# A graph attention layer and a multi-head attention layer on one core: layer 0's transformation from seven products of quarters, on normalized aggregates, with statistics on ScalarE and GpSimd

## The chip, the cores and the metric

The kernel runs on one core of a Trainium2 chip. The metric is the device time of one execution in microseconds (us). Before the change it is 2976.44 us, the median of 3 runs (2975.86 to 2976.45). The hardware profiler took one more execution, and all durations of rows in this text come from that one. The engines are TensorE (PE; its weight loads are PEld), VectorE (DVE), ScalarE (ACT), GpSimd (POOL) and SyncE (SP), which issues most DMAs.

## What is computed

`x` has 64 groups of 256 tokens with 512 features; `adj` is one 256 x 256 mask for all groups. Two layers follow each other, each on a normalized input and added to `x`:

```python
h = jnp.maximum(_layernorm(x, axis=-1), 0.0)
x = x + _L0_gnn_ref(h, adj, L0_gnn_W, L0_gnn_a_src, L0_gnn_a_dst)
h = jnp.maximum(_layernorm(x, axis=-1), 0.0)
x = x + _L1_gnn_ref(h, adj, L1_gnn_Wq, ..., L1_gnn_bo)
```

Layer 0 is a graph attention: `Wh = h W`, logits `leaky(Wh a_src + Wh a_dst)` between all pairs of tokens of a group, masked, softmax over the neighbours, times `Wh`. Layer 1 is multi-head attention with 8 heads of 64: projections with bias, scores scaled by 1/8, the same mask, softmax, values, output projection with bias. All is float32.

## The kernel before, in words

**Groups and stages.** The kernel works on one group (two token tiles of 128 tokens, `NT` = 2) at a time in each stage, and on several groups at once in different stages. Stages are Python generators; each `yield` ends a step. A hand-written list, `period` (L766) with `second` (L762), says in which order the steps of the stages are issued; it is run once per group `i`, and beside each stage stands how many groups ahead of `i` (or behind it) the step works. Every engine executes its instructions in the order in which they were issued, so this list is the order of the work on PE, VectorE, ScalarE, GpSimd and on SP's queue. Waits between engines follow from the data. The first period (`first`, L787), the steps ahead of it (L772 to L786) and `last` (L769) are written out too. The tiles of PSUM are eight banks, used in turn (`bank`, L139).

**Layer 0.** `normalize0` (two groups ahead, four steps): ScalarE sums x and the squares (L414, L420), VectorE scales the sums and adds epsilon (L417, L104), GpSimd raises to the power -0.5 (L106), VectorE forms the shift (L427), ScalarE normalizes and applies ReLU (L429); then VectorE multiplies with the two folded vectors `wa` and sums (L436), which gives the two terms of the logits. `weights0` (two steps): PE transposes one term over all rows (`pe`, L450), ScalarE takes two exponentials for the two branches of the leaky ReLU (L457, L458); then VectorE takes their maximum (L462), and GpSimd multiplies by the mask (`em`, L464) and adds the two halves (`esum`, L466). `aggregate0` (four steps): PE multiplies h by the weights (`pu`, L479) into the transposed aggregate, ScalarE copies it to `uT` (L486); in a third step PE sums `esum` over partitions (`ps`, L492), in a fourth VectorE takes the reciprocal `rs` (L496, L497). `transform0` (one group ahead, called W in the list, four steps, two per token tile): PE multiplies `uT` by the whole w (`po`, L508: per token tile four matmuls of 512 columns, each in two passes, so 8 rows), VectorE scales by `rs` and adds to x (L525).

**Layer 1.** `normalize1` (N1, three steps): VectorE's statistics (L99, L100, L104), GpSimd's power (L106), VectorE's shift (L540), ScalarE's normalization into `xn` (L545). `transpose1` (X1): PE transposes (`pt`, L561), ScalarE applies ReLU (L562), and GpSimd forms four sums of quarters, `hs` (`combine`, L165 to L168). `project_qk` (K), `project_v` (V) and `output` (O) each take seven products of quarters of the two operands in place of eight (`products`, L171). One product of K is 8 matmuls of 128 columns with two passes each; one of V or O is two matmuls of 256 columns with two passes each, hence 4 rows. VectorE adds each product to its destinations (`add_up`, L189; for O L727 straight to x, in pieces of 1024, 768, 256, 512, 512, 256 and 256 elements per partition). `attention` (A for group i, A_OLD for the one behind) has eight steps: scores of two head pairs (`psc`, L627) with ScalarE's exponential (L635); mask of one pair (VectorE: two multiplications L640 and a sum `sm` L642); mask of the other; values (`pav`, L652) with ScalarE's copy; the same four for the other two head pairs. The last of them also lets GpSimd add the bias to x (L671), sums over partitions (`psm`, L679), takes the reciprocal (`rc`, L687) and issues eight small DMAs on SP that spread it over partitions. `scale` multiplies by it on VectorE (L704) and forms the sums of quarters `as` on GpSimd.

**The order around the change**, `second` from L762:

```python
        second = [
            K, O, A_OLD, A, E0, W, W, N1, V, E0, W, W, N1, V, V, N1, A, V, A,
            U0, V, V, U0, V, X1, X1, X1, U0, U0, A, A, (scale, -1),
        ]
```

E0 is `weights0`, U0 is `aggregate0`, both two groups ahead; `aside` puts steps of one-time checks (`constants`, among them the Gram products L333) between the others during the start.

Of the kernel before, what the change touches and what calls it, by code (L numbers as in the profile page):

```python
# [28 lines left out]
def kernel(  # L29
# [72 lines left out]
    def inverse_std(var, nm, small, scale=1.0):  # L102
        ve = small.tile([P, NT], F32, tag="ve", name=f"ve{nm}")
        nc.vector.tensor_scalar(ve, var, scale, EPS, op0=ALU.mult, op1=ALU.add)  # L104
        rstd = small.tile([P, NT], F32, tag="rstd", name=f"rstd{nm}")
        nc.gpsimd.tensor_tensor(rstd, ve, minus_half, op=ALU.pow)  # L106
        return rstd
# [24 lines left out]
    def bounded():  # L132
# [6 lines left out]
        def bank(shape, name):  # L139
            return ps_mm.tile(shape, F32, tag="mm", name=name)  # L140
# [90 lines left out]
        w_sb = weights.tile([P, DC, D], F32, tag="w_sb", name="w_sb")  # L231
        nc.sync.dma_start(w_sb, w.rearrange("(c p) e -> p c e", p=P))
# [4 lines left out]
        nc.gpsimd.dma_start(adj_sb, adj.rearrange("(c p) m -> p c m", p=P))  # L237
        load_group(1)
# [13 lines left out]
        def node_weights():  # L252
            wa_c = weights.tile([P, 2, DC], F32, tag="wa_c", name="wa_c")
            for c in range(DC):
                for j in range(2):
                    junk = work.tile([P, D], F32, tag="junk", name=f"junk_a_{j}_{c}")
                    nc.vector.scalar_tensor_tensor(
                        junk, w_sb[:, c, :], 1.0, a_rows[j], op0=ALU.mult, op1=ALU.mult,
# [143 lines left out]

        nodes, edges, sums0, lefts, norms, qkv, vs, outs = {}, {}, {}, {}, {}, {}, {}, {}

        def normalize0(g):
# [5 lines left out]
            nmean = small.tile([P, NT], F32, tag="nmean", name=f"nmean_{g}")  # L411
            ssq = small.tile([P, NT], F32, tag="ssq", name=f"ssq_{g}")
            for t in range(NT):
                nc.scalar.activation(  # L414
                    h[:, t, :], xt[:, t, :], AF.Copy, accum_out=nmean[:, t : t + 1]
                )
            nc.vector.tensor_scalar_mul(nmean, nmean, -1.0 / D)  # L417
            yield
            for t in range(NT):
                nc.scalar.activation(  # L420
                    h[:, t, :], xt[:, t, :], AF.Square, bias=nmean[:, t : t + 1],
                    accum_out=ssq[:, t : t + 1],
                )
            rstd = inverse_std(ssq, f"0_{g}", small, 1.0 / D)
            yield
            nmr = small.tile([P, NT], F32, tag="nmr", name=f"nmr_{g}")
            nc.vector.tensor_mul(nmr, nmean, rstd)  # L427
# [13 lines left out]
            nc.vector.tensor_scalar_mul(edl, ed, NEG_SLOPE)  # L441
# [3 lines left out]
        def weights0(g):  # L445
# [21 lines left out]
            edges[g] = em, esum  # L467
            yield

        def aggregate0(g):  # L470

            h = nodes.pop(g)[0]
            em, esum = edges.pop(g)
            uT = big.tile([P, DC, TOK], F32, tag="uT", name=f"uT_{g}")
            for dp in range(0, DC, 2):
# [10 lines left out]
                nc.scalar.copy(uT[:, dp : dp + 2, :], pu)  # L486
                yield

            rs = small.tile([P, NT], F32, tag="rs", name=f"rs_{g}")
            ps = bank([P, NT], f"ps_{g}")  # L490
            for t in range(NT):
                nc.tensor.matmul(  # L492
                    ps[:, t : t + 1], esum[:, t * P : (t + 1) * P], ones[:, 0:1], start=True, stop=True
                )
            yield
            nc.vector.tensor_scalar_max(rs, ps, 1e-38)  # L496
            nc.vector.reciprocal(rs, rs)  # L497


            sums0[g] = uT, rs  # L500
            yield

        def spread(ps, shape):
            return ps[:, 0:HD].unsqueeze(1).to_broadcast(shape)

        def project_half(dst, left, w_t, t, n):
            for c in (2 * n, 2 * n + 1):
                nc.tensor.matmul(  # L508
                    dst, left(c, t), w_t[:, c, :], start=(c == 0), stop=(c == DC - 1)
                )  # L510

        def transform0(g):

            xt = xts[g]
            uT, rs = sums0.pop(g)

            def left(c, t):
                return uT[:, c, t * P : (t + 1) * P]

            for t in range(NT):  # L520
                po = bank([P, D], f"po0_{g}_{t}")
                project_half(po, left, w_sb, t, 0)
                yield
                project_half(po, left, w_sb, t, 1)
                nc.vector.scalar_tensor_tensor(  # L525
                    xt[:, t, :], po, rs[:, t : t + 1], xt[:, t, :], op0=ALU.mult, op1=ALU.add
                )
                yield

        def normalize1(g):  # L530
            xt = xts[g]
            mv = small.tile([P, NT, 2], F32, tag="mv", name=f"mv1_{g}")
            for t in range(NT):
                token_stats(mv[:, t, :], xt[:, t, :], f"1_{g}_{t}", small)
                if t == 0:
                    yield
            rstd = inverse_std(mv[:, :, 1], f"1_{g}", small)
            yield
            nmr = small.tile([P, NT], F32, tag="nmr1", name=f"nmr1_{g}")
            nc.vector.scalar_tensor_tensor(  # L540
                nmr, mv[:, :, 0], -1.0, rstd, op0=ALU.mult, op1=ALU.mult
            )
            norms[g] = big.tile([P, NT, D], F32, tag="xn", name=f"xn_{g}")
            for t in range(NT):
                nc.scalar.activation(  # L545
                    norms[g][:, t, :], xt[:, t, :], AF.Identity,
                    bias=nmr[:, t : t + 1], scale=rstd[:, t : t + 1],
                )
            yield
# [17 lines left out]
        def project_qk(g):  # L567
# [6 lines left out]
            s2 = work.tile([P, 4, P], F32, tag="s2", name=f"s2_{g}")  # L574

# [3 lines left out]
            def read(n, ps):  # L579
# [6 lines left out]
                elif n == 4:  # L586
# [5 lines left out]
                    ps = p5  # L592
# [119 lines left out]
        def output(g):  # L712
            xt = xts.pop(g)
            a, s = outs.pop(g)
            quarters = xt.rearrange("p t (j d) -> p (t j) d", j=2)
# [296 lines left out]
```

## Time and profile before

| What | Value |
|---|---|
| median of the runs | 2976.44 us |
| the profiled execution | 2976.81 us |
| its span, first to last instruction | 2975.0 us |
| granted clock of TensorE, mean | 0.997 of full speed |
| VectorE busy | 2162.9 us (73%) |
| ScalarE busy | 1108.7 us (37%) |
| GpSimd busy | 907.0 us (30%) |
| transform of layer 0 on PE (L508) | 460.5 us, 1024 rows |
| VectorE's masks (L640) | 459.0 us, 512 rows, mean 937 ns |
| VectorE's shift of layer 0 (L427) | 72.2 us, 64 rows, mean 1129 ns |

The page gives for each engine the busy time, and for groups of instructions the source line, the operation, the tiles written and read, the count, and the mean duration of one. A timeline gives start, duration, engine, line and tiles of each instruction or of several alike in a row, and in brackets the idle time of the engine just before, with what ended it. A row of a matmul [...]overlaps the next row; so the time that a piece of PE work takes is read from start to start. A float32 matmul shows as two rows of MATMUL.

### The profile page before, as it was taken

Reading aid. Unit: us, or ns where it says so; the run is one execution under the profiler, and the core shown is the slowest. Engines: PE = TensorE matmul, PEld = TensorE weight load, DVE = VectorE, ACT = ScalarE, POOL = GpSimd, SP = SyncE. Lnnn points to the kernel's source line nnn. Section 1 sums busy time; section 2 is a strip of 40 time slices with the busy share of each in tenths; the row PEclk is TensorE's granted clock in tenths of the full one; section 3 lists DMA queues with packets and bytes.
Section 4 is the critical chain, followed back from the end, with each engine's and each line's share of the span. In section 5 each row is a group of like instructions: output and inputs, shape, how many; then the busy total and the mean of one; then the engine's idle time right before and its main releaser. Section 6 shows DMA issues by size and latency. Waiting matters only on the chain.

```text
span 2975.0 us, 48278 instructions
## 1 busy us (share of the span) xinstructions
PE 2930.9 (99%) x18942; PEld 2334.5 (78%) x18942; DVE 2162.9 (73%) x3858; ACT 1108.7 (37%) x2523; POOL 907.0 (30%) x920
## 2 busy tenths in 40 slices
PE   7999999999999999999999999999999999999997
PEld 5778778778788787787787787887877877878875
DVE  5777777777777777777777777777777777777766
ACT  4433434334343333334343333433333343433321
POOL 2223323223233233233232232332332332322322
PEclk9999999999999999999999999999999999999999
DMA  3121221221212212212212212122122122122122
GB/s 128 22 43 23 42 41 25 43 35 31 43 31 34 44 29 36 43 22 44 38 28 43 35 31 43 31 35 43 29 36 43 22 43 36 29 43 33 25 29 37
DMA packets 82714, 111.21 MB, mean 37 GB/s; under 512 B 11826, under 2 KB 48690, under 8 KB 82482
## 3 DMA queue, kind: packets, MB, share of 16 engines
q1 hardware_dynamic: 81682, 105.95, 22.3%
q8 instruction: 152, 2.49, 0.3%
q0 software_dynamic: 800, 2.11, 0.2%
q14 instruction: 80, 0.66, 0.1%
HBM read 40.90 MB, written 33.55 MB: 25 GB/s over the span
## 4 chain that ended last, share of the span: by engine, by line
PE 97%; DVE 2%; DMA 1%; POOL 0%; SPq 0%; issue 0%; ACT 0%; DVEq 0%; POOLq 0%
PE pqk L216 27%; PE po L508 15%; PE po L207 13%; PE pv L207 13%; PE psc L627 8%; PE pav L652 8%; PE pu L479 7%; PE psm L679 2%; PE pt L561 2%; PE pe L450 1%; PE ps L492 1%; DVE ex L640 0%; PE pgram L333 0%; DMA a_row<-in_L_gnn_a_dst_dram 0%; SPq L692 0%
## 5 line engine op out<-in xcount | busy, mean ns | idle before, releaser
L640 DVE TENSOR_TENSOR ex<-ex,maskT 128x512 f32<-128x512 f32 x512 | 459.0, 937 | 86.7 <-ACT ex L635 86.7
L508 PE MATMUL po<-w_sb,uT 128*128 128x512 f32 x1024 | 460.5, 592 | 0.0
L464 POOL TENSOR_TENSOR em<-e,maskT 128x512 f32<-128x512 f32 x64 | 81.0, 1265 | 1045.7 <-DVE e L462 1040.1
L525 DVE SCALAR_TENSOR_TENSOR x<-po,rs,x 128x512 f32<-128x512 f32 x128 | 96.1, 751 | 369.8 <-PE po L508 369.8
L508 PEld LDWEIGHTS po<-w_sb,uT 128*128 128x128 f32 x1024 | 189.6, 190 | 187.7 <-issue 184.1
L635 ACT ACTIVATE ex<-psc 128x512 f32<-128x512 f32 x512 | 264.4, 603 | 125.4 <-PE psc L627 125.4
L727 DVE TENSOR_TENSOR x<-po,x 128x256 f32<-128x256 f32 (+3 forms) x448 | 305.8, 683 | 6.7 <-PE po L207 6.5
L216 PEld LDWEIGHTS pqk<-hs,wq_sb 128*128 128x128 f32 x2048 | 268.3, 192 | 13.6 <-POOL hs L166 0.8
L216 PE MATMUL pqk<-hs,wq_sb 128*128 128x128 f32 x2048 | 270.0, 275 | 0.7 <-POOL hs L166 0.7
L216 PE MATMUL pqk<-hs,wk_sb 128*128 128x128 f32 x2048 | 270.5, 275 | 0.0
L207 PE MATMUL po<-wo_sb,as 128*128 128x256 f32 x1024 | 265.2, 382 | 4.4 <-POOL as L166 4.4
L660 ACT COPY aT<-pav 128x512 f32<-128x512 f32 x128 | 75.1, 587 | 514.6 <-PE pav L652 486.8
L207 PE MATMUL pv<-wv_sb,hs 128*128 128x256 f32 x1024 | 262.7, 379 | 0.0
L652 PE MATMUL pav<-ex,v 128*64 128x256 f32 x2048 | 251.6, 386 | 6.8 <-DVE ex L640 3.7
L627 PE MATMUL psc<-qk 64*128 64x256 f32 x2048 | 255.7, 389 | 0.0
L216 PEld LDWEIGHTS pqk<-hs,wk_sb 128*128 128x128 f32 x2048 | 249.3, 192 | 0.0
L479 PE MATMUL pu<-em,h 128*128 128x256 f32 x1024 | 243.2, 381 | 3.5 <-POOL em L464 3.5
L545 ACT ACTIVATE xn<-x,nmr,rstd 128x512 f32<-128x512 f32 x128 | 97.2, 806 | 389.7 <-DVE nmr L540 389.7
L627 PEld LDWEIGHTS psc<-qk 64*128 64x128 f32 x2048 | 187.3, 186 | 67.7 <-ACT aT L660 25.9
L207 PEld LDWEIGHTS pv<-wv_sb,hs 128*128 128x128 f32 x1024 | 194.9, 190 | 53.5 <-issue 29.9
L106 POOL TENSOR_TENSOR rstd<-ve,minus_half 128x2 f32<-128x2 f32 x128 | 90.4, 706 | 460.0 <-DVE ve L104 459.9
L165 POOL TENSOR_TENSOR hs<-hT 128x256 f32<-128x256 f32 x64 | 78.7, 1229 | 479.5 <-ACT hT L562 479.5
(166 smaller groups left out, 5252.3 us busy)
## 6 DMA issues: line engine op xcount, KB each, us to landing
x<-in_x_dram SPq DMA_DIRECT2D x64, 512.0 KB, 5.4
rb<-rc SPq DMA_DIRECT2D x512, 64.0 KB, 4.7
out_dram<-x SPq DMA_DIRECT2D x128, 256.0 KB, 2.0
w_sb<-in_L_gnn_W_dram SPq DMA_DIRECT2D x1, 1024.0 KB, 8.2
wq_sb<-in_L_gnn_Wq_dram SPq DMA_DIRECT2D x4, 256.0 KB, 13.4
wk_sb<-in_L_gnn_Wk_dram SPq DMA_DIRECT2D x4, 256.0 KB, 9.9
wo_sb<-in_L_gnn_Wo_dram SPq DMA_DIRECT2D x4, 256.0 KB, 6.6
wv_sb<-in_L_gnn_Wv_dram SPq DMA_DIRECT2D x4, 256.0 KB, 6.6
```

The lines of the kernel that those rows point to most:

```text
L106: nc.gpsimd.tensor_tensor(rstd, ve, minus_half, op=ALU.pow)
L207: nc.tensor.matmul(dst[:, 0:HD], left[:, c, :], wt[:, slot, c, :], start=c == 0, stop=c == 1)
L216: nc.tensor.matmul(dst[:, at : at + P], wt[:, slot, c, e * P : (e + 1) * P], left[:, c, :], start=c == 0, stop=c == 1,)
L479: nc.tensor.matmul(pu[:, d, :], h[:, m, (dp + d) * P : (dp + d + 1) * P], em[:, m, :], start=(m == 0), stop=(m == NC - 1),)
L508: nc.tensor.matmul(dst, left(c, t), w_t[:, c, :], start=(c == 0), stop=(c == DC - 1))
L525: nc.vector.scalar_tensor_tensor(xt[:, t, :], po, rs[:, t : t + 1], xt[:, t, :], op0=ALU.mult, op1=ALU.add)
L545: nc.scalar.activation(norms[g][:, t, :], xt[:, t, :], AF.Identity, bias=nmr[:, t : t + 1], scale=rstd[:, t : t + 1],)
L627: nc.tensor.matmul(psc[r][:, m, :], qk[rows, 2 + e % 2, m * P : (m + 1) * P], qk[rows, e % 2, :], start=True, stop=True,)
L635: nc.scalar.activation(ex[:, r, :, :], psc[r], AF.Exp, scale=SCALE)
L640: nc.vector.tensor_mul(ex[:, r, :, :], ex[:, r, :, :], maskT)
L652: nc.tensor.matmul(pav[r * DH : (r + 1) * DH, i, :], v[j][:, m, at : at + DH], pair[i][:, r, m, :], start=(m == 0), stop=(m == NC - 1),)
L727: nc.vector.tensor_add(dst, spread(ps, [P, dst.shape[1], HD]), dst)
```

## The change

- **Transformation from seven products.** `w_sb` is held as quarters (`load_quarters`) with their sums (`combine_w(w_sb)`), `aggregate0` ends with GpSimd's four sums of quarters of `uT` (`us`), and `transform0` runs `products` with `product_rows`, as O does; it has seven steps. `add_to_rows` is O's addition, now shared. The whole w, for the folded vectors, goes to two tiles that later hold `hT` and `xn`; w is thus loaded twice.
- **Normalized aggregates.** The row sum (`ps`) and its reciprocal `rs` are a third step of `weights0`; a fourth step transposes `rs` over all rows (`prs`) and ScalarE copies that to `rb0`. VectorE multiplies `pu` by `rb0` where ScalarE copied before.
- **Statistics.** A class `Stats` sums x (scaled by -1/D) and squares on ScalarE, and takes epsilon, power and shift on GpSimd. Both layers use it. `edl` goes to GpSimd.
- **Order.** W has seven steps, E0 four; masks 2 and 3 of the group behind (A_OLD) go from the start of the period to between the products K; the addition of K's product 4 waits until that of product 5 (`held`).

The core of the diff:

```diff
-        w_sb = weights.tile([P, DC, D], F32, tag="w_sb", name="w_sb")
-        nc.sync.dma_start(w_sb, w.rearrange("(c p) e -> p c e", p=P))
+        w_c = [big.tile([P, 2, D], F32, tag=tag, name=f"w_{tag}") for tag in ("hT", "xn")]
+        for i in range(2):
+            nc.sync.dma_start(w_c[i], w[i * HD : (i + 1) * HD, :].rearrange("(c p) e -> p c e", p=P))
...
+        w_sb = load_quarters(w, "w_sb")
         load_group(1)
...
+        class Stats:
...
+            def mean(self, t):
+                nc.scalar.activation(
+                    self.junk[:, t, :], self.xt[:, t, :], AF.Copy, scale=-1.0 / D,
+                    accum_out=self.nmean[:, t : t + 1],
+                )
+            def squares(self, t):
+                nc.scalar.activation(
+                    self.junk[:, t, :], self.xt[:, t, :], AF.Square, bias=self.nmean[:, t : t + 1],
+                    accum_out=self.ssq[:, t : t + 1],
+                )
+            def close(self):
...
+                nc.gpsimd.tensor_scalar(ve, self.ssq, 1.0 / D, EPS, op0=ALU.mult, op1=ALU.add)
+                nc.gpsimd.tensor_tensor(rstd, ve, minus_half, op=ALU.pow)
+                nc.gpsimd.tensor_tensor(nmr, self.nmean, rstd, op=ALU.mult)
+                return nmr, rstd
...
             nc.gpsimd.tensor_tensor(esum, em[:, 0, :], em[:, 1, :], op=ALU.add)
-            edges[g] = em, esum
+            yield
+            ps = bank([P, NT], f"ps_{g}")
+            for t in range(NT):
+                nc.tensor.matmul(
+                    ps[:, t : t + 1], esum[:, t * P : (t + 1) * P], ones[:, 0:1], start=True, stop=True
+                )
+            rs = small.tile([P, NT], F32, tag="rs", name=f"rs_{g}")
+            nc.vector.tensor_scalar_max(rs, ps, 1e-38)
+            nc.vector.reciprocal(rs, rs)
+            yield
+            pr = bank([P, N], f"prs_{g}")
+            for t in range(NT):
+                nc.tensor.transpose(
+                    pr[:, t * P : (t + 1) * P], rs[:, t : t + 1].to_broadcast([P, P]), ident
+                )
+            rb0 = work.tile([P, N], F32, tag="rb0", name=f"rb0_{g}")
+            nc.scalar.copy(rb0, pr)
+            edges[g] = em, rb0
             yield
...
-                nc.scalar.copy(uT[:, dp : dp + 2, :], pu)
+                nc.vector.tensor_mul(
+                    uT[:, dp : dp + 2, :], pu, rb0.unsqueeze(1).to_broadcast([P, 2, N])
+                )
...
+            sums0[g] = a, combine(a, ("us", str(g)))
+            yield
...
         def transform0(g):
+            a, s = sums0.pop(g)
+            yield from products(
+                a, s, f"po0_{g}", partial(product_rows, w_sb), partial(add_to_rows, xts[g])
+            )
...
         def normalize1(g):
+            stats = Stats(xt, xn, f"1_{g}")
+            stats.mean(1)
+            stats.squares(1)
+            yield
+            stats.mean(0)
+            stats.squares(0)
+            nmr, rstd = stats.close()
+            yield
...
         second = [
-            K, O, A_OLD, A, E0, W, W, N1, V, E0, W, W, N1, V, V, N1, A, V, A,
-            U0, V, V, U0, V, X1, X1, X1, U0, U0, A, A, (scale, -1),
+            N0, A_OLD, A, E0, W, W, W, V, E0, A, W, W, V, E0, W, N1, W, E0, N1, V, V, A, U0, N1,
+            V, V, U0, V, X1, X1, X1, A, A, (scale, -1),
         ]
         period = [
-            (load, 3), A_OLD, K, A_OLD, O, K, N0, O, K, N0, O, K, N0, O, K, O, N0, K, O,
+            (load, 3), K, O, K, N0, O, (aggregate0, 1), K, N0, O, K, A_OLD, O, K, N0, O, A_OLD, K, O,
+            K, O,
         ] + second
```

## The prediction, made before the change was run

> **What bounds the kernel now.** I first read the page's busy times and its chain of waits.
>
> ```profile
> PE 2930.9 (99%) x18942; PEld 2334.5 (78%) x18942; DVE 2162.9 (73%) x3858; ACT 1108.7 (37%) x2523; POOL 907.0 (30%) x920
> ...
> PE 97%; DVE 2%; DMA 1%; POOL 0%; SPq 0%; issue 0%; ACT 0%; DVEq 0%; POOLq 0%
> ```
>
> The reader is to see that TensorE (PE) is busy from end to end and that the chain that ended last is PE for 97%. A busy PE can hide small gaps, so next comes PE's timeline over one period, from one group's last value product (`pav`) to the next group's.
>
> ```profile
> 1427.27 1.95 PE L652 MATMUL pav<-ex,v 128*64 128x256 f32 x16
> ...
> 1432.08 0.43 PE L450 MATMUL pe<-ident,es 128*128 128x128 f32 x2
> 1432.35 3.60 PE L508 MATMUL po<-w_sb,uT 128*128 128x512 f32 x8
> 1435.79 1.03 PE L207 MATMUL pv<-wv_sb,hT 128*128 128x256 f32 x4
> 1436.65 3.60 PE L508 MATMUL po<-w_sb,uT 128*128 128x512 f32 x8
> 1440.08 1.03 PE L207 MATMUL pv<-wv_sb,hs 128*128 128x256 f32 x4
> ...
> 1472.58 1.95 PE L652 MATMUL pav<-ex,v 128*64 128x256 f32 x16
> ```
>
> A period is 1472.58 - 1427.27 = 45.31 us, and no row between carries an idle time: PE waits for nobody. 64 periods are 2900 us; some 75 us are start and tail. Starts minus starts give what a piece takes: a transform of one token tile 1435.79 - 1432.35 = 3.44 us, a product of quarters (4 matmuls of 256 columns) 1436.65 - 1435.79 = 0.86, the two transposes `pe` 0.27.
>
> Last, the other engines, because the change hangs new PE work on them. VectorE's timeline:
>
> ```profile
> 1437.60 0.66 DVE L462 TENSOR_TENSOR e<-e,e 128x512 f32<-128x512 f32 x1
> ...
> 1459.93 1.22 DVE L727 TENSOR_TENSOR x<-po,x 128x1024 f32<-128x1024 f32 x1
> 1461.07 0.68 DVE L192 TENSOR_TENSOR s<-qk,pqk 128x512 f32<-128x512 f32 x1
> 1461.66 0.16 DVE L417 TENSOR_SCALAR nmean<-nmean 128x2 f32<-128x2 f32 x1
> 1461.73 0.95 DVE L727 TENSOR_TENSOR x<-po,x 128x768 f32<-128x768 f32 x1
> 1462.60 0.68 DVE L194 TENSOR_TENSOR qk<-qk,pqk 128x512 f32<-128x512 f32 x1
> ```
>
> and GpSimd's (POOL):
>
> ```profile
> 1438.34 1.27 POOL L464 TENSOR_TENSOR em<-e,maskT 128x512 f32<-128x512 f32 x1 [16.73 <-DVE e L462]
> 1439.68 0.72 POOL L466 TENSOR_TENSOR esum<-em 128x256 f32<-128x256 f32 x1
> ```
>
> VectorE starts the next row about 0.08 us before a row ends: an addition to four quarters takes 1.14 us of its time, to three 0.87, 512 elements 0.60, 256 0.33. From the start of the maximum (L462) to the end of `esum` are 1440.40 - 1437.60 = 2.80 us. Today PE asks for `esum` only at 1449.59, nine microseconds later.
>
> **What the Trainium skill says.** "SBUF — State Buffer", section "Who interferes with whom": a VectorE instruction with two SBUF inputs and a GpSimd instruction that reads SBUF exclude each other for the whole instruction. The trace agrees:
>
> ```profile
> 2213.20 1.29 DVE L640 TENSOR_TENSOR ex<-ex,maskT 128x512 f32<-128x512 f32 x2
> ...
> 2220.62 1.83 DVE L704 TENSOR_TENSOR aT<-aT,rb 128x512 f32<-128x512 f32 x2
> 2220.63 1.27 POOL L165 TENSOR_TENSOR hs<-hT 128x256 f32<-128x256 f32 x1 [7.55 <-ACT hT L562]
> ```
>
> Two such multiplications alone take 1.29 us; beside GpSimd's addition they take 1.83 (0.54 more), and that addition takes 1.27 where it takes 0.73 undisturbed. "TensorE: Matmul & The Clock Gate", section "Step-by-step: what each phase is for": only weight loads are pulled ahead, matmuls stay in program order. So one matmul that waits holds all behind it. No row here contradicts it.
>
> **The change part by part.**
>
> *Transform (L508 out, seven products in).* PE loses 3.44 + 3.43 = 6.87 us a period and gains 7 x 0.865 = 6.06. VectorE loses the two L525 rows and gains seven additions like L727's.
>
> *Normalization of the aggregate.* Two more transposes per group (`pr`) cost PE 0.27 like `pe`. The new multiplication out of PSUM is priced as L196's 0.68 and replaces ScalarE's copy of 0.57; ScalarE gains a 256-column copy (0.37, as L609). Net for PE: -6.87 + 6.06 + 0.27 = **-0.54 us a period**, 63 periods: -34 us.
>
> *Statistics of layer 1 on ScalarE:* two rows of 0.65 + 0.22 and two of 0.72 + 0.19 per group, 3.5 us. ScalarE goes from 17.2 to about 20 us of a period, no bound. The chain is: last addition to x, four statistics with the `rb0` copy among them (3.5), three small GpSimd steps, two normalizations (1.52), transposes `pt`. GpSimd's power takes 0.70; the other two steps have no row, so I bound each by a tiny GpSimd row (0.1) and the power (0.7) and take 0.5; with hand-overs 2.0. Then `xn` is there some 7.3 us after `pr` starts; `pt` begins 8.1 us after it. Hidden by five V products and two `pu`; slack 0.8, and if the lower bounds hold 1.6. If the cover is gone it costs up to 0.7 a period, which I keep for the range.
>
> *Smaller steps.* The combination `us` is four more GpSimd additions (0.73 to 1.17 each, 3 to 4.7 us), issued after `hs` and `as` with nine K and O products and more before W1 reads it: nothing. GpSimd's `edl` delays only the `bo_b` additions, done 6.5 us into the period. Masks 2 and 3 go into the K products, away from `hs` and `as`: VectorE gets back about 3 us that the lock took, off the path. The addition that waits for `p5` goes behind K5 and no longer blocks VectorE (2.06 us idle before L198 today): off the path too.
>
> *Row sums pulled forward.* This sets the end. `ps` and `pr` now stand in the middle of W. I count from the start of `pav` (0). PE: W0 starts at 1432.35 - 1427.27 = 5.08, and after W0 W1 W2 V0 W3 W4 V1 (7 x 0.865) PE reaches `ps` at 11.14. VectorE is free by then (its reciprocal `rc` ends at 5.1) and follows W0, whose result is there at 6.15: W0 to 7.29, W1 to 8.16, W2 to 8.50, maximum to 9.10 with its end at 9.16. GpSimd starts `em` at 9.24; alone, `esum` would be there at 9.24 + 2.06 = 11.30, and with the weight load (0.19) and hand-over `ps` would run at 11.54: 0.40 late. But right behind the maximum stand mask 0's two multiplications and a sum (two SBUF inputs each). The first starts at 9.10 and holds the port when `em` comes. In the trace the two engines then alternate. I take 0.41 more for `em` (the 0.54 seen, less the 0.13 that the multiplication has run): end 10.92; the second multiplication from 10.87; `esum` +0.43: end 12.14; `ps` at **12.38, 1.24 late**. Then `sm` to 12.7, W3 13.3, W4 13.9, V1 14.23, the two small steps for `rs` 14.6, weight load 0.14: `pr` can start at 14.78. PE, itself late, reaches it at 12.38 + 0.43 + 1.73 = 14.54: **0.24 more**. Behind the waiting `ps` are queued W5, W6 and all of V; VectorE and ScalarE wait with them, so nothing catches up within the period. Sum: 1.48 us in each of the 62 periods that have a group two ahead: +92 us.
>
> *Start.* One more MB stands on SP's queue ahead of x1 and the query weights. These were issued from 2.3 us on and took 13.4 us to land; the first Gram product, at 19.86, needs them. w's own MB took 8.2 us, so they come 2 to 3 us after PE wants them. Seven products with `us`, the combination of w (4 x 0.6) and GpSimd's short steps, with nothing to hide them, take some 4 to 5 us longer than two transforms and their statistics. Together +7 (bounds 2 and 12). The tail changes nothing that I can price: 0.
>
> **Sum.** 2975.0 + 7 - 34 + 92 = 3040 us of span. The profiled execution took 2976.81, 1.8 more than its span; the median of the runs is 2976.44, 0.4 below that. So 3041, given as **3040 us**, 2.1% slower. About 0.2% is what a measurement can tell here from no change.
>
> **Rivals.**
> - *The row sums are ready in time* (faster). If mask 0 were done before the maximum's result is needed, or if the additions of W lagged less, `esum` would come before 11 and PE would keep only its gain: 2975 + 7 - 34 = 2948, median about 2949. Its place is the wait of `ps`; it decides if the chain W0-to-`esum` takes under 5.0 us from W0's end at 6.11. For it: PE has no idle time today, and W's additions fit VectorE's 12 idle us a period. Against it: the rows alone add up to 1.14 + 0.87 + 0.34 + 0.74 + 2.06 = 5.15, before a lock or the weight load. Chance 0.11.
> - *No lock:* 0.40 late at `ps`, `pr` in time: 62 x 0.40 = 25, so 2974. For it, `em` has been alone in all 64 rows (1258 to 1269 ns). Against it, mask 0 now stands beside it. Chance 0.15.
> - *VectorE keeps the port* for all three rows: `em` from 10.95, `esum` to 13.0, `ps` 2.1 late, `pr` in time: 62 x 2.1 = 130, 3079; a late `xn` on top ends as high. Against it, the alternation seen. Chance 0.17.
> - *The products do not take less PE time:* seven quarters plus `pr` are 6.33 against 6.87, measured on the same shapes; I see no way to lose this, it has no chance of its own.
>
> **How the numbers follow.** Forecast 0.57 (own range 3022 to 3058: stall 1.2 to 1.75). The range reaches down past "no lock" with the bounds of the start, 2965, and up to VectorE first, 3080; left out are the fast case (0.11) and the upper half of the slowest (0.09). Faster by over 0.2% (under 2970.5): the fast case and the low part of "no lock", 0.15; within 0.2%: 0.08; slower: 0.77.
>
> **What would show it.** A period of 46.2 us on PE's timeline; idle time of PE before `ps`, released by GpSimd's `esum`, near 1.2, and before `pr`, released by VectorE's `rs`, near 0.2; `em` at some 1.7 us instead of 1.27, `esum` at 1.15 instead of 0.72; mask 0's rows at 1.1 or more. No idle time before `pt`, `pu` or K. Wrong if PE's timeline shows no wait at `ps`: then 44.77 us a period and the fast case. Wrong in size if `em` is undisturbed, or if `pt` waits for `xn`.

## The result, and the profile after

The changed kernel takes 3072.34 us, the median of 4 runs (3070.26 to 3075.14). That is 1.0323 of the time before, with an interval of 1.0305 to 1.0341. The profiled execution took 3075.14 us, with a span of 3073.4 us: 98.4 us more than before.

The page's busy times and chain of waits:

```profile
PE 2938.6 (96%) x19838; PEld 2486.6 (81%) x19838; DVE 2138.0 (70%) x3670; ACT 1240.8 (40%) x2971; POOL 1070.1 (35%) x1496
...
PE 78%; DVE 17%; issue 2%; DMA 1%; POOL 0%; SPq 0%; ACT 0%; DVEq 0%; POOLq 0%; ACTq 0%
```

TensorE's busy time is nearly that of before (2930.9 us), but its share of a longer span fell from 99% to 96%, and VectorE now stands in the chain with 17%. PE waits. The waits by line (total us, times, longest) name the two places:

```profile
PE ps L496 <- POOL esum L491: 65.7, 63, 3.8
...
PE prs L505 <- DVE rs L501: 13.0, 63, 0.5
```

Neither pair appears among PE's waits before. One period of PE's timeline, from one group's last `pav` to the next group's:

```profile
1446.23 1.95 PE L683 MATMUL pav<-ex,v 128*64 128x256 f32 x16
...
1458.50 0.61 PE L496 MATMUL ps<-ones,esum 128*128 128x1 f32 x4 [0.98 <-POOL esum L491]
1458.96 1.11 PE L207 MATMUL po<-w_sb,uT 128*128 128x256 f32 x4
1459.91 1.03 PE L207 MATMUL po<-w_sb,us 128*128 128x256 f32 x4
1461.13 0.40 PE L505 MATMUL prs<-ident,rs 128*128 128x128 f32 x2 [0.20 <-DVE rs L501]
...
1492.66 1.95 PE L683 MATMUL pav<-ex,v 128*64 128x256 f32 x16
```

A period is 46.43 us, against 45.31 before. `ps` starts 12.27 us after the first `pav`. The products ahead of it are done 11.12 us after it (the last one starts at 1456.48 and takes 0.865), so `ps` is 1.15 late. From the second of the two `po` rows to `prs` are 1.22 us where a product takes 0.86: 0.36 late.

What held `esum` up stands on VectorE in the same stretch:

```profile
1454.90 0.68 DVE L487 TENSOR_TENSOR e<-e,e 128x512 f32<-128x512 f32 x1
1455.50 2.36 DVE L671 TENSOR_TENSOR ex<-ex,maskT 128x512 f32<-128x512 f32 x2
...
1458.91 1.47 DVE L550 TENSOR_TENSOR x<-po,x 128x512 f32<-128x512 f32 x2
...
1460.63 0.15 DVE L500 TENSOR_SCALAR rs<-ps 128x2 f32<-128x2 f32 x1
```

and on GpSimd:

```profile
1455.67 1.65 POOL L489 TENSOR_TENSOR em<-e,maskT 128x512 f32<-128x512 f32 x1 [3.25 <-DVE e L487]
1457.39 1.05 POOL L491 TENSOR_TENSOR esum<-em 128x256 f32<-128x256 f32 x1
```

The reader is to see two engines working through the same three microseconds, each slower than alone: the two masks take 2.36 us (1.29 alone), `em` 1.65 (1.27) and `esum` 1.05 (0.72). Their rows end in turn: the first mask at 1456.19, `em` at 1457.31, the second mask at 1457.86, `esum` at 1458.44, `sm` (the sum of the two masks' results, L673) at 1458.99. `ps` follows `esum` at once. `rs` comes late through VectorE's order: mask 0 has pushed back two additions to x and one of V, which stand ahead of `rs` and fill VectorE from 1458.91 on.

**Where the 98.4 us lie.** The first `psm` of each group marks the periods. In us from the start of the span:

| | first | second | third | last |
|---|---|---|---|---|
| before | 110.87 | 160.72 | 206.02 | 2944.19 |
| after | 136.83 | 194.26 | 240.70 | 3043.82 |

Up to the second `psm` 33.5 us are lost, from there to the last 66.1, and the tail gives 1.3 back. The steady part is what the timeline above shows. The start is a story of its own, on PE's timeline:

```profile
26.61 1.22 PE L335 MATMUL pgram<-b_q 128*128 128x128 f32 x4 [3.28 <-DMA b_q<-in_L_gnn_Wq_dram]
...
32.03 5.25 PE L522 MATMUL pu<-em,h 128*128 128x256 f32 x16
...
52.28 2.04 PE L345 MATMUL pgram<-gram 128*128 128x128 f32 x8 [6.03 <-DVE gram L341]
...
59.20 2.07 PE L306 MATMUL pbias<-b_o,bv_c 128*128 128x256 f32 x4 [2.35 <-DMA b_o<-in_L_gnn_Wo_dram]
...
142.27 0.29 PE L475 MATMUL pe<-ident,es 128*128 128x128 f32 x1 [2.44 <-DVE junk L461]
...
155.47 1.01 PE L496 MATMUL ps<-ones,esum 128*128 128x1 f32 x4 [3.77 <-POOL esum L491]
```

The first `pt` comes at 62.71 where it came at 46.04. The Gram products wait 3.28 us for `b_q`, a quarter of the query weights that GpSimd loads. GpSimd issued that load like this before

```profile
8.85 0.74 POOL L295 DMA_DIRECT2D b_q<-in_L_gnn_Wq_dram  x1
```

and like this after:

```profile
20.21 0.23 POOL L466 TENSOR_SCALAR edl<-ed 128x2 f32<-128x2 f32 x1 [11.63 <-DVE junk L461]
20.38 0.80 POOL L297 DMA_DIRECT2D b_q<-in_L_gnn_Wq_dram  x1
```

`edl`, which the change gave to GpSimd, now stands ahead of the load in GpSimd's order and waits 11.63 us for VectorE's logits. From issue to landing `b_q` takes 6.2 us (6.8 before), so the late issue is what makes it late. The extra MB on SP's queue is not seen at this place: PE starts on the quarters of wq that come from that queue at 19.71, without a wait (19.86 before). No run moves `edl` alone.

Layer 0's first transform waits 2.23 for `us`. VectorE forms the sums of the query and key weights (L157 to L160, eight rows of 0.69, from 44.73 to 49.8) ahead of the last additions to x and of the Gram copies, so PE waits 6.03 at 52.28 where it waited 2.94. In the second period the one-time checks stand ahead of VectorE's logits (L461); at one of them VectorE idles 1.66 us until the load of `b_v` lands, and more checks stand between the logits and the maximum; `pe` and `ps` wait.

And a wait can cost twice. The rows of `pu` that stand at 32.03, as minimum, median and maximum in ns, and a later stretch with busy times of PE, PEld, VectorE, ScalarE and GpSimd and the granted clock (third column from the end):

```profile
L522 PE MATMUL pu<-em,h x16: 379/460/634, 32.0 to 36.9; 128*128 128x256 f32 x16
```

```profile
52.20:56.00 3.80, 3.71 (x13) 3.39 (x14) 0.53 (x3) 2.40 (x8) 1.08 (x3) 0.52 0.00 0
```

The first rows of `pu` take 634 ns and the last 379, and from the start of one row to the next are 0.427 us up to 35.3 and 0.216 from there on: 16 rows fill 5.09 us where they filled 3.46 before. After the wait of 6.03 us the granted clock is 0.52, and the eight Gram rows take 1.84 us where they took 0.97. This is what the Trainium skill says in "TensorE: Matmul & The Clock Gate", section "Part 1: The HAM clock gate (the "warmup" mystery)": after an idle window TensorE gets half its clock until it has been busy for some microseconds. The trace agrees. For the stretch of `pu` the clock column shows 1.00, but only because this trace's record of the clock begins at 35.34 us, where the rows become fast; in "row sums later" below, whose record begins earlier, the column shows 0.50 over the same slow rows (30.30 to 32.90).

Counted against the rows of before, the rows of the start take longer by 1.0 us at the Gram products from 26.61 on, 1.6 at `pu`, 3.4 from 52.28 to 62.71, 1.6 from 75.76 to 82.64, 1.7 from 143.81 on and 3.0 from 155.47 on: some 12 us, where the kernel before lost about 1.7 to half the clock (from 127.4 on). Not all of that is lost time: 1.7 of the 3.4 stand ahead of PE's wait for `b_o`, which GpSimd issues at 56.03 behind its steps of the statistics, so that this wait would only have been longer. How much of the 33.5 us the slow rows make up was not measured. In the steady periods the clock is 1.00; waits of 0.98 and 0.20 us don't lower it. These stretches fall differently from execution to execution: six executions here whose instructions are the same up to the first `pt` have it between 59.25 and 63.17 us.

### The profile page after: what moved, and what is told of

It is laid out like the page before. It is cut to its first block, busy times and chain, and to the rows that moved or that the text cites. A ratio compares the mean times of both kernels' runs of the same rounds, so it can differ in the third digit from the quotient of the medians.

```text
span 3073.4 us, 51612 instructions
## 1 busy us (share of the span) xinstructions
PE 2938.6 (96%) x19838; PEld 2486.6 (81%) x19838; DVE 2138.0 (70%) x3670; ACT 1240.8 (40%) x2971; POOL 1070.1 (35%) x1496
## 4 chain that ended last, share of the span: by engine, by line
PE 78%; DVE 17%; issue 2%; DMA 1%; POOL 0%; SPq 0%; ACT 0%; DVEq 0%; POOLq 0%; ACTq 0%
PE pqk L216 26%; PE po L207 14%; PE pv L207 9%; PE psc L658 8%; PE pav L683 8%; PE pu L522 7%; DVE x L550 7%; DVE ex L671 5%; DVE sm L673 2%; PE psm L710 2%; PE pt L588 2%; DVE e L487 1%; PE prs L505 1%; DVE s2v L192 1%; PE pe L475 1%
## 5 line engine op out<-in xcount | busy, mean ns | idle before, releaser
L550 DVE TENSOR_TENSOR x<-po,x 128x256 f32<-128x256 f32 (+3 forms) x896 | 604.4, 687 | 492.5 <-PE po L207 472.4
L671 DVE TENSOR_TENSOR ex<-ex,maskT 128x512 f32<-128x512 f32 x512 | 397.4, 818 | 0.0
L466 POOL TENSOR_SCALAR edl<-ed 128x2 f32<-128x2 f32 x64 | 14.6, 227 | 927.2 <-DVE junk L461 927.2
L207 PE MATMUL po<-w_sb,us 128*128 128x256 f32 x1024 | 254.4, 381 | 2.2 <-POOL us L166 2.2
L617 ACT ACTIVATE p<-pqk,bias 128x128 f32<-128x128 f32 x256 | 73.0, 368 | 435.2 <-PE pqk L216 435.2
L415 ACT ACTIVATE xn<-x 128x512 f32<-128x512 f32 x128 | 80.5, 629 | 397.4 <-DVE x L550 397.4
L207 PEld LDWEIGHTS po<-w_sb,us 128*128 128x128 f32 x1024 | 195.4, 191 | 29.8 <-POOL us L166 2.6
L216 PEld LDWEIGHTS pqk<-hT,wq_sb 128*128 128x128 f32 x1536 | 196.2, 191 | 27.8 <-ACT ex L666 20.9
L522 PEld LDWEIGHTS pu<-em,h 128*128 128x128 f32 x1024 | 196.2, 192 | 26.9
```

What stands on the lines that cost most here:

```text
L207: nc.tensor.matmul(dst[:, 0:HD], left[:, c, :], wt[:, slot, c, :], start=c == 0, stop=c == 1)
L216: nc.tensor.matmul(dst[:, at : at + P], wt[:, slot, c, e * P : (e + 1) * P], left[:, c, :], start=c == 0, stop=c == 1,)
L415: nc.scalar.activation(self.junk[:, t, :], self.xt[:, t, :], AF.Copy, scale=-1.0 / D, accum_out=self.nmean[:, t : t + 1],)
L522: nc.tensor.matmul(pu[:, d, :], h[:, m, (dp + d) * P : (dp + d + 1) * P], em[:, m, :], start=(m == 0), stop=(m == NC - 1),)
L550: nc.vector.tensor_add(dst, src, dst)
L617: nc.scalar.activation(p5[:, c, :], ps[:, c, :], AF.Identity, bias=bias10[:, c : c + 1])
```

## The experiments

All edits are made to the changed kernel; the table at the end gathers the times. The first question is whether the steady loss is the early row sums and nothing else.

**Row sums later.** The two steps of `weights0` that make PE wait go back behind the products of W and V.

```diff
-            N0, A_OLD, A, E0, W, W, W, V, E0, A, W, W, V, E0, W, N1, W, E0, N1, V, V, A, U0, N1,
-            V, V, U0, V, X1, X1, X1, A, A, (scale, -1),
+            N0, A_OLD, A, E0, W, W, W, V, E0, A, W, W, V, W, N1, W, E0, N1, V, V, V, E0, A, U0, N1,
+            V, U0, V, X1, X1, X1, A, A, (scale, -1),
```

> The changed kernel with one thing moved in its order: the row sum ps is issued behind the last product of W, and the transposes pr behind three more products V; nothing is left out. Theory (PE stalls at ps and pr because the row sums are asked for too early): both waits vanish from PE's timeline, the period goes from 46.43 us to the sum of its PE pieces, 44.77, and 62 periods give back 103 us: about 2970. Rival (the wait only moves: pu, pt or the banks wait instead, or the additions of the seven products lag whatever the order): the period stays above 46 and the time above 3040. Second rival (the products of quarters do not take less PE time): a period of 45.3 without any wait, about 3004.

Measured: 2970.63 us, 0.9983 of the kernel before (0.9976 to 0.999). PE's timeline:

```profile
1440.40 1.95 PE L683 MATMUL pav<-ex,v 128*64 128x256 f32 x16
...
1453.25 0.50 PE L496 MATMUL ps<-ones,esum 128*128 128x1 f32 x4
...
1456.29 0.38 PE L505 MATMUL prs<-ident,rs 128*128 128x128 f32 x2
...
1485.21 1.95 PE L683 MATMUL pav<-ex,v 128*64 128x256 f32 x16
```

The period is 44.81 us, and no idle time stands at `ps` or `prs`. `em` still takes 1.65 us and `esum` 1.05: the lock is there as before, and costs nothing because nobody waits for its end. So the whole steady loss was the place of two steps, and without it the change saves 0.50 us a period (45.31 before).

**Mask 0 later.** One step of A moves behind the step that forms `rs`; the row sums stay early.

```diff
-            N0, A_OLD, A, E0, W, W, W, V, E0, A, W, W, V, E0, W, N1, W, E0, N1, V, V, A, U0, N1,
+            N0, A_OLD, A, E0, W, W, W, V, E0, W, W, V, E0, A, W, N1, W, E0, N1, V, V, A, U0, N1,
```

> The changed kernel with mask 0 issued behind the row sum's reciprocal instead of straight behind the maximum; ps and pr stay where they are, nothing is left out. Theory (two causes: the chain from W0 to esum is too long by 0.4 us by itself, and mask 0 beside em adds the rest through the shared port, and delays rs through VectorE's order): em back to 1.27 us, esum to 0.72, PE's wait at ps from 1.16 down to about 0.4, none at pr, a period of 45.2, about 2997. Rival (no lock, only VectorE's order): em stays at 1.65, the wait at ps stays at 1.16 and only that at pr goes: 46.1, about 3052. Rival (the lock is all of it): no wait at ps either, 44.8, about 2972.

Measured: 3009.04 us, 1.0109 (1.0092 to 1.0126), 12 us above the expectation; the period is 45.35. GpSimd and then PE:

```profile
1425.63 1.27 POOL L489 TENSOR_TENSOR em<-e,maskT 128x512 f32<-128x512 f32 x1 [3.23 <-DVE e L487]
1426.98 0.72 POOL L491 TENSOR_TENSOR esum<-em 128x256 f32<-128x256 f32 x1
```

```profile
1427.75 0.60 PE L496 MATMUL ps<-ones,esum 128*128 128x1 f32 x4 [0.28 <-POOL esum L491]
```

Without mask 0 beside them both GpSimd rows are back at their times alone, and `prs` no longer waits, since nothing of mask 0 stands ahead of `rs`. That it is the masks and not just any work of VectorE shows here too: two additions to x, one input of which lies in PSUM, run beside `em` and `esum` (from 1425.79 and 1426.65), and neither is slower. `ps` starts 11.56 us after `pav` (1416.19), 0.44 late. So the 1.15 us split into 0.44 of the bare chain from W0 to `esum` and 0.71 that came with mask 0, which is what `em` (0.38) and `esum` (0.33) had lost; the 0.36 at `prs` came with mask 0 too. Of the 12 us missed, 0.15 us a period (9 us) is the period, which was expected at 45.2.

**Statistics of layer 1 on VectorE**, the rest unchanged.

```diff
...
-            stats.mean(1)
-            stats.squares(1)
...
+            token_stats(mv[:, 1, :], xt[:, 1, :], f"1_{g}_1", small)
...
-            nmr, rstd = stats.close()
...
+            rstd = inverse_std(mv[:, :, 1], f"1_{g}", small)
...
+            nc.vector.scalar_tensor_tensor(
+                nmr, mv[:, :, 0], -1.0, rstd, op0=ALU.mult, op1=ALU.mult
+            )
```

> The changed kernel with layer 1's statistics on VectorE as before the change, at the same steps; nothing is left out. Theory (that part of the change lies off PE's path): the period stays at 46.43 within 0.1 us; about 3072. Rival (ScalarE's four statistics hold up rb0 or xn and so PE): the period gets shorter by some tenths of a us, 3050 or less. Rival (VectorE is near its limit): the two extra rows of 0.7 us delay W6's addition and V, and the period gets longer, 3100 or more.

Measured: 3074.59 us in one run; the period is 46.43, the same to a hundredth. VectorE is busy 114 us longer over the span (2252.2 against 2138.0) and ScalarE 181 us shorter, and PE does not notice. In the steady periods this part of the change is off the path.

**Masks back ahead of K.** A_OLD's two masks return to the start of the period, beside `hs` and `as`.

```diff
-            (load, 3), K, O, K, N0, O, (aggregate0, 1), K, N0, O, K, A_OLD, O, K, N0, O, A_OLD, K, O,
-            K, O,
+            (load, 3), A_OLD, K, A_OLD, O, K, N0, O, (aggregate0, 1), K, N0, O, K, O, K, N0, O, K, O,
+            K, O,
```

> The changed kernel with one part undone in its order: masks 2 and 3 of the group behind at the start of the period again, beside GpSimd's hs and as; nothing is left out. Theory (that move is off PE's path): the mean mask multiplication goes from 0.82 back to above 0.9 us, GpSimd's as from 0.73 back to about 1.17, the period stays at 46.4 us and the time within 4 us of 3072. Rival (the move freed VectorE where it counts): a period of 46.7 or more, 3090 or more. Rival (the move costs, because the masks stand ahead of the last K additions and so of normalize0's last step): a shorter period, 3060 or less.

Measured: 3070.69 us in one run, period 46.43. The group of the masks on the page (busy us, mean ns):

```profile
L671 DVE TENSOR_TENSOR ex<-ex,maskT 128x512 f32<-128x512 f32 x512 | 515.7, 1047 | 178.1 <-ACT ex L666 178.1
```

The masks' mean rises from 818 to 1047 ns, and the four additions `as` from 0.73 to between 1.06 and 1.21 us. The move thus does free VectorE and GpSimd of each other, and the period does not depend on it. The first `psm` comes 5.0 us earlier in this one execution, 3.5 of which are there at the first `pt` already, where the instructions are still the same.

The other experiments ask where the start's 33.5 us come from. Each of the next three has one theory; since the changed kernel's own runs lie between 3070.26 and 3075.14, the time of a single run tells little, and the place of the `psm` is read.

**One-time work denser and elsewhere.** The sums of `wv` and `wo` move off VectorE's busy places, and the checks go only between the steps ahead of W.

```diff
-                if i == 0 and n == len(first):
+                if i == 0 and n == 8:
                     combine_w(wv_sb)
-                if i == 1 and n == 8:
+                if i == 1 and n == len(period) - 1:
                     combine_w(wo_sb)
                 step(stage, g)
-                if i and n % 2:
+                if i and n % 2 and n < 20:
                     aside()
```

> The changed kernel with VectorE's one-time work moved: the sums of wv's quarters into the first period's K products, those of wo to the end of the second period, and the one-time checks only among the K products; nothing is left out. Theory (some 10 us of the loss beyond the steady periods come from this work standing ahead of the last step of normalize0, for which pe and all of W now wait): no wait of 2 us at pe in the first two periods, ps of the second waits 1.2 instead of 3.8; the second psm comes about 10 us earlier than 194.3, and the time falls by as much, to about 3062. Rival (the start is lost to the loads and to PE's clock): the second psm comes at most 3 us earlier.

Measured: 3072.13 us in one run. The second `psm` is 6.0 us earlier (188.25), not 10, and the span ends only 3.0 earlier. `ps` in the second period now waits 0.52 in place of 3.77, but `pe` still waits 2.67 and 1.08 there. That the checks hold `ps` up is shown. That they also hold `pe` is not shown by this edit, which left the cause in place: a check that waits 1.89 us for the load of `b_v` still stands right ahead of the logits. The other 3 us are not the edit's: 1.6 of them lie in the last full period, where value products behind a wait of 1.5 us for `xn` run at half the clock (0.50 from 2994.2 to 2997.5, rows of 634 ns) and in the changed kernel, behind the same wait, do not; three periods are longer by 0.3 each, and the tail by 0.4.

**Query and key sums later.** `prepare_qk()` moves behind the copies of the Gram products.

```diff
-        prepare_qk()
         steps((transform0, 0), (transform0, 0), (transform0, 0), (normalize1, 0), (transform0, 0))
         step(normalize1, 0)
         aside(2)
+        prepare_qk()
```

> The changed kernel with the sums of wq's and wk's quarters on VectorE (about 5 us) taken from between the third and the fourth product of the first group's W and put behind that group's statistics and Gram steps; nothing is left out. Theory (at the start the additions to x wait for these sums, and statistics, output bias and the first K product wait for x): the first psm comes 5 us earlier than 136.8. Rival (the start is set by the loads, or by the DMA of the output bias, which is issued behind the statistics anyway): 0 to 1 us.

Measured: 3071.23 us in one run; the first `psm` is at 133.44, 3.4 us earlier and not 5, which by itself is within what one start differs from another. `pt`, at 57.12, lies 2.1 us ahead of the earliest without the edit. The wait for the Gram copies falls from 6.03 to 0.81, as the theory says. But the next wait grows from 2.35 to 5.04: the load of `b_o` has not landed, since GpSimd issues it behind its steps of the statistics (at 50.23). A part of a removed wait was taken over by the one behind it.

**Gram products later.** The first `aside()`, which issues them, moves behind layer 0's transform.

```diff
-        aside()
         steps((normalize0, 1), (weights0, 0), (normalize0, 1), (weights0, 0), (weights0, 0))
...
         step(normalize1, 0)
+        aside()
         aside(2)
```

> The changed kernel with the first Gram products (for the one-time checks) taken from ahead of the first group's row sums and aggregation and put behind its W products, where PE is idle for 6 us; nothing is left out. Theory (the late query weights make PE wait 3.3 us there, after which it runs the aggregation of 16 rows in 5.1 us instead of 3.5): the aggregation starts 5 to 6 us earlier and the first psm comes about 7 us earlier than 136.8. Rival (the chain through VectorE's sums and the output bias sets the start, and what comes earlier on PE waits there): 0 to 2 us.

Measured: 3067.26 us in one run; the first `psm` is at 128.95, 7.9 us earlier (7 expected), and `pt` at 55.24, 4.0 ahead of the earliest without the edit. The wait for `b_q` is gone and `pu` starts at 26.18. But `pu` still fills 4.89 us: PE now waits 4.68 for the first `esum` just ahead of `ps`. So the Gram products together with their late load were what delayed `pu`; that the load also slowed `pu` is not shown: the slow rows come without it too, behind another wait.

**Checks spread thin.** As "one-time work", but one check every eighth step.

```diff
-                if i and n % 2:
+                if i and n % 8 == 7:
                     aside()
```

> As the run with the one-time work moved, but the one-time checks are spread thinly over the first five periods (one step in eight) instead of standing among the K products of the second, where VectorE still waited for a load ahead of normalize0's last step; nothing is left out. Theory (what delays the second period is one-time work ahead of normalize0's last step on VectorE): no wait over 1 us at pe in the second period, and the second psm comes 8 to 10 us earlier than 194.3; the time falls by about as much. Rival (it only moves the stalls to later periods): the second psm is early but the time stays within 3 us of 3072.

Measured: 3083.39 us in one run, 11 us *worse* than the changed kernel; the theory missed. PE's timeline:

```profile
140.48 1.19 PE L335 MATMUL pgram<-b_k 128*128 128x128 f32 x4 [6.13 <-DMA b_k<-in_L_gnn_Wk_dram]
...
207.25 1.01 PE L496 MATMUL ps<-ones,esum 128*128 128x1 f32 x4 [7.47 <-POOL esum L491]
```

and VectorE's, ahead of that `ps`:

```profile
199.62 0.68 DVE L374 SCALAR_TENSOR_TENSOR junk_b<-brow 1x512 f32<-1x512 f32 x1 [3.62 <-DMA brow<-in_L_gnn_bq_dram]
```

Stretched over more periods, a check falls onto places where its load is issued only as PE comes to need it (`b_k` is issued by GpSimd at 134.79, and PE waits 6.13 us), or where VectorE itself waits for a check's load while W's additions and the maximum stand behind it (3.62 us for `brow`, and 7.47 at `ps`). The first `psm` is 7.5 us earlier (129.37), with fewer checks ahead of it, the third 5.7 later (246.35).

**All together, checks spread thin**, and in the first period too the row sums later (the diff of "row sums later", those of the three start experiments with the thin spread, and this):

```diff
-            (load, 3), K, (normalize0, 1), K, (weights0, 1), K, N0, (weights0, 1), N0, K, (weights0, 1),
-            (weights0, 1), K, (aggregate0, 1), (aggregate0, 1), N0, K, (aggregate0, 1), K,
+            (load, 3), K, (normalize0, 1), K, (weights0, 1), K, N0, (weights0, 1), N0, K, K,
+            (weights0, 1), K, (weights0, 1), (aggregate0, 1), (aggregate0, 1), N0, K, (aggregate0, 1),
```

> The changed kernel with the row sums later (as in the first run of this study, also in the first period), the sums of wq and wk later, the Gram products later and the one-time checks spread; nothing is left out. Theory (steady loss and start loss add up from separate causes): 2970.6 less 5, 7, 9 and 2, about 2948, 0.9% below the kernel before. Rival (the start has a floor of its own, set by the loads): 2960 to 2968.

Measured: 2962.01 us, 0.9957 of the kernel before (0.994 to 0.9973), 14 us above the expectation. The first `psm` is at 110.52, as early as before the change, but the second and third are at 170.34 and 224.13: the thin checks again, with 6.19 us for `b_k`.

**All together, checks dense**: the same with the checks of "one-time work".

```diff
-                if i and n % 8 == 7:
+                if i and n % 2 and n < 20:
```

> As the combined run, with the one-time checks among the K products of the second period again instead of spread over five; nothing is left out. Theory (spreading them is what cost the combined run 15 us: a wait of 6 us for a load ahead of Gram products on PE, and two late W phases): psm of the third period at about 206 instead of 224, and 2962 less 16 is about 2946. Rival (any place for the checks costs the same, only in other periods): within 4 us of 2962.

Measured: 2951.02 us, 0.9915 of the kernel before (0.9899 to 0.9932). The page:

```profile
PE 2899.2 (98%) x19838; PEld 2487.1 (84%) x19838; DVE 2135.1 (72%) x3670; ACT 1240.3 (42%) x2971; POOL 1069.8 (36%) x1496
...
PE 96%; DVE 1%; DMA 1%; POOL 1%; SPq 0%; ACT 0%; issue 0%; DVEq 0%; POOLq 0%; ACTq 0%
```

The chain is PE for 96% again, the period 44.80, the second `psm` at 166.82. Of the start's 33.5 us order alone gives back 27.4 (6.5 of them come with "row sums later" by itself, whose second `psm` is at 187.76); 6.1 stay. It is the fastest version here.

| Kernel | us | runs | first, second, third `psm` |
|---|---|---|---|
| changed kernel | 3072.34 | 4 | 136.83, 194.26, 240.70 |
| row sums later | 2970.63 | 18 | 134.83, 187.76, 232.56 |
| mask 0 later | 3009.04 | 4 | 136.57, 193.63, 238.98 |
| statistics on VectorE | 3074.59 | 1 | 136.56, 192.88, 239.32 |
| masks back | 3070.69 | 1 | 131.82, 189.15, 235.58 |
| one-time work | 3072.13 | 1 | 136.58, 188.25, 235.01 |
| query and key sums later | 3071.23 | 1 | 133.44, 189.67, 236.11 |
| Gram products later | 3067.26 | 1 | 128.95, 185.34, 231.78 |
| checks spread thin | 3083.39 | 1 | 129.37, 190.38, 246.35 |
| all, checks thin | 2962.01 | 4 | 110.52, 170.34, 224.13 |
| all, checks dense | 2951.02 | 4 | 116.58, 166.82, 211.94 |

## Why the prediction was right, and where its size was off

The direction and the mechanism hold: PE waits for `esum`, and behind the waiting `ps` stands everything else. The time was forecast at 3040 us (2965 to 3080), and is 32 more. It lies above the range of the forecast's own case (3022 to 3058), and inside the whole range only because that reaches up to the case "VectorE keeps the port", which did not come about. The mechanism of the steady periods is right; that the total still falls inside is luck, because what the start lost on top happens to stay within the room that this case had added. By the steps of the prediction:

- **Transform and transposes, -0.54 us a period: right.** Without the waits the period is 44.81, against 44.77 by the sum.
- **`ps` 1.24 late, `prs` 0.24 more: right.** Measured 1.15 and 0.36, 1.51 together against 1.48. The count from `pav` holds step by step: `em` was to start at 9.24 and did at 9.44, to end at 10.92 and did at 11.09; `esum` was to end at 12.14 and did at 12.21. "Mask 0 later" shows that the two causes are the ones named. "No lock" was wrong by the lock's 0.7 us, and "VectorE keeps the port" because the engines alternate.
- **The period, 46.25: 0.18 short.** 0.04 is the sum without waits and 0.03 the stall. Most of the rest lies at `ps`: it occupies PE for 0.46 us after a wait, and for 0.37 in "row sums later", where it does not wait; I priced no row higher for standing behind a wait. From the second `psm` on the loss is 66.1 us; for this stretch the forecast gives about 56 (60 stalls of 1.48, less 61 savings of 0.54).
- **Edits priced at nothing: right in the steady periods.** The two experiments that undo one each leave the period at 46.43. `us`, `edl` and the held addition were not undone one by one, but the 0.04 us above is all that is left for them together. `xn` is ready at 1468.05 and `pt` starts at 1469.14, a slack of 1.1 where 0.8 was forecast. GpSimd's short steps take 0.26 and 0.20 us, not 0.5 each, but the power takes 1.16 there and not 0.70, so that the three come to about what was priced. At the start `edl` was not free (next point).
- **"Start. ... Together +7 (bounds 2 and 12)": mis-sized.** Measured +33.5 up to the second `psm`, far outside the bounds. With two of the stalled periods, which lie in this stretch, the forecast for it is about 9, so some 25 of the 33 us that the profiled execution lies above its sum are here. The unhidden `us` was there (2.23). The wait for the query weights has the size that was forecast (3.28 us, 2 to 3), but by luck: it is not the extra MB on SP's queue but GpSimd's `edl`, ahead of the issue of `b_q`, that made them late. "GpSimd's `edl` delays only the `bo_b` additions" is thus wrong at the start. Three more things failed. First, I priced the added work on PE's own sequence, but during the start PE waits for VectorE: the sums of weights, the Gram copies and the checks stand in its queue ahead of the additions and logits, and the new order moved W, N0 and the row sums to places behind them (6.03, 2.44 and 3.77 us of PE's waits). That order is what costs is shown by the last experiment, in which 27.4 us come back; it moves the row sums and the Gram products' load as well, so that it does not give VectorE's queue a share of its own. Second, the row sums of group 1, in the first period, stall PE too (1.82 and 0.55 us), and the sum counted only the groups behind it. Third, I took durations from a steady PE; behind the waits of the start rows ran at half the clock and took some 12 us longer in this execution, part of it ahead of waits that hid it.
- **Tail 0:** measured -1.3.

What stays open: of what the last 6.1 us at the start consist, what `edl` by itself costs there, and how much the half clock does. The single moves at the start have one run each, and the same start differs by up to 3.9 us between executions; so the sum of the moves (27.4 us, in a kernel timed in several runs) is shown, and the share of each is not.

## What to carry to other kernels

When a step is pulled forward on an engine that executes in order, write out the chain that feeds it with start times, and put in what stands beside each link on a shared port; here such a count told a stall of 1.5 us per period to within 0.03, and moving two steps of a list turned a loss of 3.2% into a gain of 0.2%. Price the start of a kernel by the queue of the engine that holds the one-time work, not by the work that is added to the bound engine. When a step moves to another engine, look at what that engine issues behind it: here a load of weights left GpSimd 11.5 us later. Add to a wait of several microseconds the slow rows that can come behind it. Spreading one-time work thin was no safer here than keeping it dense: each piece needs a place where its load has landed and nothing urgent stands behind it.

## What the hardware showed that was not expected

- GpSimd's steps on 128x2 elements are short: a multiply-add with constants 0.19 us, a product 0.20, the power 0.70. Beside VectorE's sum `sm`, which has two SBUF inputs, the power took 1.16.
- Sixteen rows of 256 columns fill 3.46 us of PE at full clock. Behind waits of 3 to 5 us they fill 4.80 to 5.53 in nine of eleven executions, with 0.427 and then 0.216 us from row to row. In "statistics on VectorE" and "masks back" the same rows, behind the same waits, all took 379 to 382 ns: there the trace has its half-clock stretch, 3.41 us long, earlier, and it is over (at 29.95 and 29.60) before `pu` starts. Once half the clock came behind a wait of only 1.5 us, in "one-time work".
- VectorE with two SBUF inputs and GpSimd alternate instruction by instruction. Both lose: GpSimd 0.38 and 0.33 us on two rows, VectorE 1.07 on two masks. An addition with one input in PSUM took nothing from GpSimd ("mask 0 later": `em` 1.27, `esum` 0.72). This fits "SBUF — State Buffer", section "Who interferes with whom", and "mask 0 later" removes it.
